# Folding layer 1's output weights in its first step, with the first queries made one item earlier

## The chip, the cores and the metric

The kernel runs on one core of a Trainium2 chip. The metric is the device time of one execution in microseconds (us). The engines are named as in the profile: PE is TensorE (matrix products), DVE is VectorE, ACT is ScalarE, POOL is GpSimd, SP is SyncE, which issues most of the DMA transfers. Each engine works through its own queue of instructions in order, and engines wait for each other through semaphores. PEclk is the clock that the throttle granted to TensorE, 1.00 being full speed.

## The reference

Two transformer layers on x of shape 2 x 1024 x 256, all in float32. Layer 0 is a 16-head attention with a ternary-weight FFN beside it. Layer 1 is a latent attention with its own FFN beside it; only that attention matters here. Cut to its core:

```python
q = rmsnorm(x @ wq_a.T) @ wq_b.T            # 16 heads: 128 plain + 64 rotated values
ckv = x @ wkv_a.T
kv, k_pe = rmsnorm(ckv[..., :64]), apply_rope(ckv[..., 64:])
w = wkv_b.reshape(16, 256, 64)
q_absorb, out_absorb = w[:, :128], w[:, 128:]
q_abs = einsum('bhsd,hdc->bhsc', q_nope, q_absorb)
scores = (q_abs @ kv + apply_rope(q_pe) @ k_pe) * SCALE    # causal softmax -> attn
x = einsum('bhst,btc->bhsc', attn, kv)
x = einsum('bhsc,hdc->bhsd', x, out_absorb)
return x.reshape(b, s, 16 * 128) @ wo.T
```

The last two products take no input but weights beside `x`, so `out_absorb` and `wo` can be multiplied with each other first, for each head: a 64 x 256 matrix. In the same way `wq_b` can be multiplied with `q_absorb`. The kernel calls this folding.

## The kernel before, in words

**Layers.** Layer 0 and everything that prepares layer 1 run under an order written out by hand. A list `fill` holds the pieces of the two FFNs, and a list `side` holds the pieces that prepare layer 1. The loop at L1076 takes one piece of `fill` and then one or more pieces of `side`, until both are empty. Each piece issues its matmuls and the copies that empty its PSUM bank. The pieces of `fill` that stand last are the FFN's products `up` (matmul L679) and `down` (twelve matmuls at L696 into one bank, which DVE adds to x at L701). Their banks come from a ring of three, `ps_m`, which the pieces of `side` use too.

**Preparation.** Among the pieces of `side` are, in this order near the end:

- `fold(p)` for the head pairs p = 0..7 (L818). Its loads come from SP two pieces ahead (`fold_load`, L799). Four matmuls at L825 fold the query weights, two at L833 fold the output weights (eight records in the profile for the first, four for the second); the results are copied out of two banks of `ps_m` by `copy_out`, which takes DVE and ACT in turn.
- `turn_keys` (L779), then `queries1` (L784), which turns four blocks of query latents with four matmuls at L791 and scales them on DVE at L792, out of one bank of `ps_m`.
- `query(k)` for k = 0, 1 (L1098), the queries of layer 1's first step. `project` (L139 and L146, 32 matmuls) writes two PSUM banks. `rotate` (L158) copies from there on ACT (L165, L153, L168), multiplies with cosine and sine (L169, L170) and adds the halves (four times L174), all of these six on POOL.

The last items of `side` are ordered as

```python
side += last[:2] + [lambda: query(0), last[2], lambda: query(1), last[3]]
```

where `last` are the four pieces of `queries1` for the second batch. Five pieces of `fill` (L696) come after the last of them.

**Layer 1's attention.** Its buffers (`att1`, and `ps1` in PSUM) lie in the memory that layer 0 leaves. It runs in 16 steps: a batch, a pair of blocks of 128 rows (i and 7 - i) and half of the heads. A step has four cycles c = 0..3. A cycle computes scores (matmul L1164, then DVE adds the mask and takes the maximum at L1171, then ACT takes the exponential at L1175), turns them over on DVE (L1181), computes a quarter of the product with the values for the step before (L1212), and in cycles 0 and 2 projects and rotates the queries of the next step. In cycles 1 and 3 come transposes (L1198) and the output product with the folded weights `wvo` (L1239) for the steps before. The first step has no step before it, so it has neither values nor output products; `wvo` is first read in the third step. PSUM holds two pairs of banks "s" for the scores and projections and four banks "o" for the values. Each step's turned weights lie in a tile `pT`, of which there are two buffers. The values need `vrep`, which 32 transfers from SP write (L1115) in x's place, after x with the first layer added has been written to memory (L703).

Of the kernel before, what the change touches and what calls it, by code (L numbers as in the profile page):

```python
# [46 lines left out]
def two_layers(ctx: ExitStack, tc: tile.TileContext, a: dict, out: bass.AP):  # L47
# [38 lines left out]
    def copy_out(dst, src, scale=None):  # L86

        turn[0] += 1
        if turn[0] % 2:
            if scale is None:  # L90
                nc.vector.tensor_copy(dst, src)
            else:
                nc.vector.tensor_scalar(dst, src, scale, None, ALU.mult)
        else:
            nc.scalar.activation(dst, src, AF.Copy, scale=1.0 if scale is None else scale)
# [94 lines left out]
    with ExitStack() as scope:  # L190
# [10 lines left out]
        def ps_bank():  # L201
            return ps0.tile([P, SC], F32, tag="m", name="ps_m", bufs=3)
# [596 lines left out]
        def fold_load(p):  # L799
            if p == 0:  # L800


                wm = main.tile([P, 2, NPAIR, P], F32, tag="wA", name="wm")
                folded["wm"], folded["w2"] = wm[:, 0], wm[:, 1]
                nc.sync.dma_start(folded["w2"][:R2], a["wpe2"])
                folded["wvo"] = main.tile([P, NPAIR, E], F32, tag="wB", name="wvo")
                folded["wo"] = l0.tile([P, 4, 2, E], F32, tag="ctx_n", name="fold_wo")
            t0 = l0t.tile([P, S], F32, tag="head0", name="fold0", bufs=3)
            t, at = {}, 0
            for key, width in (("wbn", LQ), ("wka", LKV), ("wva", LKV)):  # L810
                t[key] = t0[:, at : at + 2 * width].rearrange("p (h r) -> p h r", h=2)
                at += 2 * width
            t["wo"] = folded["wo"][:, p % 4]
            for key in ("wbn", "wka", "wva", "wo"):
                nc.sync.dma_start(t[key], a[key][:, 2 * p : 2 * p + 2, :])
            folded[p] = t

        def fold(p):  # L818
            if p + 2 < NPAIR:
                fold_load(p + 2)  # L820
            t = folded[p]
            pm = ps_bank()
            for lo, n, at in ((0, P, 0), (P, R2, P)):
                for hh in range(2):
                    nc.tensor.matmul(  # L825
                        pm[P - n :, at + hh * LKV : at + (hh + 1) * LKV],
                        t["wbn"][:, hh, lo : lo + n], t["wka"][:, hh, :], start=True, stop=True,
                    )
            copy_out(folded["wm"][:, p, :], pm[:, :P])
            copy_out(folded["w2"][R2:, p, :], pm[R2:, P : 2 * P])  # L830
            pv = ps_bank()
            for hh in range(2):
                nc.tensor.matmul(  # L833
                    pv[hh * LKV : (hh + 1) * LKV, :E], t["wva"][:, hh, :], t["wo"][:, hh, :],
                    start=True, stop=True,
                )
            copy_out(folded["wvo"][:, p, :], pv[:, :E])


        with tc.manual_schedule():  # L840

# [234 lines left out]
            while fill:  # L1076
                k = len(fill)
                pump()
                for _ in range(-(-len(side) // k)):
                    side.pop(0)()  # L1080
                if k == 17:
                    wpe = main.tile([P, 8 * E], F32, tag="wC", name="wpe")

                    maskw = wpe[:, NPAIR * P + 4 * P :]
                    trig = wpe[:, NPAIR * P : NPAIR * P + 4 * P].rearrange("p (k t) -> p k t", k=4)
                    wpe = wpe[:, : NPAIR * P].rearrange("p (r c) -> p r c", r=NPAIR)
                    nc.sync.dma_start(wpe, a["wpe"])
                    for k_, i in enumerate((TB - 1, 0)):
                        for x_, key in enumerate(("cosq", "sinq")):
                            nc.sync.dma_start(  # L1090
                                trig[:, 2 * k_ + x_], a[key][:, i * P : (i + 1) * P]
                            )

                    maskw = maskw.bitcast(BF16)
                    nc.gpsimd.memset(maskw[:, : S - P], 0.0)
                    nc.gpsimd.tensor_copy(maskw[:, S - P :], maskz[:, SC - P :])

                    def query(k):  # L1098
                        q = ready[steps[0]][k]
                        q.project(ps_pair())  # L1100
                        q.rotate(
                            room=[temp("t").rearrange("p (r t) -> p r t", r=QP) for _ in range(2)]
                        )

                    ahead(0)
                    last = [lambda c=c, n=n: queries1(1, c, n) for n in (0, 4) for c in range(2)]
                    side += last[:2] + [lambda: query(0), last[2], lambda: query(1), last[3]]
            while side:
                side.pop(0)()

# [20 lines left out]
    with ExitStack() as scope:  # L1131
# [9 lines left out]

        class Step:
            pass

        def new_step(b, i, g):
            s = Step()
# [108 lines left out]
        with tc.manual_schedule():  # L1255
            prev, older = None, None

            def values(n0, n1):
                for sb in range(n0, n1):
                    product(prev, sb)  # L1260

            for at in range(len(steps)):
                s = new_step(*steps[at])
                nxt = ahead(at + 1) if at + 1 < len(steps) else ()
                for c in range(NCY):
                    wide = [2 * c, 2 * c + 1]
                    share = (c * NSB // NCY, (c + 1) * NSB // NCY) if prev is not None else (0, 0)
                    if c == 0 and older is not None:
                        normalize(older, 0)
                        fetch_x(older)  # L1270
                    scores(s, 0, wide[:1])
                    if c == 0:
                        if older is not None:
                            normalize(older, 1)
                        if prev is not None:
                            inverse(prev)
                        scores(s, 0, wide[1:])
                        scores(s, 1, wide)
                        values(*share)
                    else:  # L1280
                        values(*share)
                        scores(s, 1, wide)
                        turn_over(s, 0, wide[0])
                        scores(s, 0, wide[1:])
                    k = c // 2
                    q, after = None, []
                    if c % 2 == 0:
                        if nxt:
                            q = nxt[k]
                            q.project(pair("t"))  # L1290
                    elif prev is not None:
                        t = pair("t")
                        if older is not None:
                            after.append(output(older, k, t[:, 0, :E]))
                        after.append(inverse_T(prev, k, t[:, 1]))
                    if c == 0:
                        turn_over(s, 0, wide[0])
                        turn_over(s, 0, wide[1])
                        turn_over(s, 1, wide[0])
                        turn_over(s, 1, wide[1])  # L1300
                    else:
                        turn_over(s, 1, wide[0])
                        turn_over(s, 1, wide[1])
                        for f in after:
                            f()
                        turn_over(s, 0, wide[1])
                    if q is not None:
                        q.rotate()
                older, prev = prev, s

            for k in range(2):
                normalize(older, k)
                if k == 0:
                    fetch_x(older)
            inverse(prev)
            mid = prev.nsb // 2
            values(0, mid)
            for k in range(2):
                t = pair("t")
                after = [output(older, k, t[:, 0, :E]), inverse_T(prev, k, t[:, 1])]  # L1320
                for f in after:
                    f()
                if k == 0:
                    values(mid, prev.nsb)
            normalize(prev, 0)
            mid = (prev.nsb + NSB) // 2
            values(prev.nsb, mid)
            t = pair("t")
            output(prev, 0, t[:, 0, :E])()
            values(mid, NSB)  # L1330
            normalize(prev, 1)
            t = pair("t")
            output(prev, 1, t[:, 0, :E])()
# [67 lines left out]
```

## Time and profile before

| | us |
|---|---|
| median of 3 runs | 1321.2 |
| lowest and highest | 1320.69, 1322.42 |
| the profiled execution, its own time | 1319.51 |
| its span, first to last instruction | 1317.4 |
| PE busy | 1268.4 (96%) |
| DVE busy | 744.2 (56%) |
| ACT busy | 641.3 (49%) |
| POOL busy | 487.2 (37%) |
| mean granted clock | 0.984 |

A line of the timeline gives the start, the duration, the engine, the line of the kernel, the operation with what it writes and reads, how many instructions it stands for, and in brackets how long the engine was idle before it and whose work ended that. A name with an arrow such as `ps_s<-kT,qc` reads "ps_s from kT and qc". A window's line gives each engine's busy time in that stretch, the granted clock, the DMA engines' mean share and their GB/s. The span counts from the first instruction; 2.1 us of the execution lie around it.

### The profile page before, as it was taken

How to read it: one execution, taken by the hardware profiler on the slowest of the kernel's cores; microseconds unless marked ns; L12 is line 12 of the kernel's file. 1: busy time of each engine (PE TensorE's matmuls, PEld its weight loads, DVE VectorE, ACT ScalarE, POOL GpSimd, SP SyncE). 2: the span in 40 equal slices, each digit the busy share in tenths (PEclk: the TensorE clock that was granted, in tenths of full speed). 3: DMA queues.
4: the chain of work that ended last, by engine and by line, in shares of the span. 5: the costliest groups of instructions: out<-in, count | busy, mean ns of one | idle time of the engine just before them, and what ended most of it. 6: DMA issues, size and time to landing. Idle time of an engine off the chain costs nothing. (4 is left out here: it accounts for less than half of the span.)

```text
span 1317.4 us, 36641 instructions
## 1 busy us (share of the span) xinstructions
PE 1268.4 (96%) x15790; PEld 797.0 (60%) x15790; DVE 744.2 (56%) x1873; ACT 641.3 (49%) x1227; POOL 487.2 (37%) x514
## 2 busy tenths in 40 slices
PE   7989999999999999999998889999999999999997
PEld 6445554544646544456576557777666667777665
DVE  5656454646555656125324567666657677666663
ACT  3455536556455433433324555555555555555541
POOL 5444315344324021113126344443444344443320
PEclk9889999999999999999999899999999999999999
DMA  7212300010101000002042200000000000000000
GB/s 227 56 41 65 104 10 17 9 25 1 25 1 25 1 25 20 17 1 78 1 130 58 32 18 11 24 13 6 27 11 26 7 27 11 26 11 6 23 6 23
DMA packets 65809, 41.12 MB, mean 31 GB/s; under 512 B 37840, under 2 KB 63184, under 8 KB 65392
## 3 DMA queue, kind: packets, MB, share of 16 engines
q1 hardware_dynamic: 64528, 35.25, 10.5%
q8 instruction: 124, 2.03, 0.6%
q0 software_dynamic: 416, 2.49, 0.5%
q10 hardware_dynamic: 704, 1.05, 0.3%
q14 instruction: 37, 0.30, 0.1%
HBM read 26.18 MB, written 10.49 MB: 28 GB/s over the span
## 5 line engine op out<-in xcount | busy, mean ns | idle before, releaser
L1175 ACT ACTIVATE p<-p,nmax 128x1024 f32<-128x1024 f32 (+7 forms) x256 | 197.2, 771 | 206.3 <-DVE nmax L1171 205.5
L1164 PE MATMUL ps_s<-kT,qc 128*128 128x512 f32 (+3 forms) x768 | 279.8, 499 | 14.2 <-DVE nmax L1171 13.0
L1171 DVE CUSTOM_DVE_ANT_0 p<-ps_s,wpe 128x1024 f32<-128x1024 f32 (+7 forms) x256 | 184.9, 744 | 185.5 <-PE ps_s L1164 180.3
L454 ACT ACTIVATE p<-ps_s 128x1024 f32<-128x1024 f32 (+1 forms) x192 | 153.3, 809 | 168.4 <-PE ps_s L447 163.3
L1164 PEld LDWEIGHTS ps_s<-kT,qc 128*128 128x128 f32 x768 | 131.4, 191 | 123.8 <-issue 90.9
L1181 DVE STREAM_TRANSPOSE pT<-p 128x1024 f32<-128x1024 f32 (+7 forms) x256 | 186.5, 758 | 13.2 <-ACT p L1175 13.2
L406 PE MATMUL ps_m<-head,head 16*128 16x512 f32 (+3 forms) x672 | 178.1, 537 | 1.7 <-DVE nmx L417 1.3
L447 PE MATMUL ps_s<-head,head 17*128 17x512 f32 (+3 forms) x768 | 166.2, 537 | 0.0
L1212 PE MATMUL ps_o<-pT,vrep 32*64 32x128 f32 x9216 | 151.3, 275 | 6.3 <-DVE xT L1222 3.7
L1212 PEld LDWEIGHTS ps_o<-pT,vrep 32*64 32x64 f32 x9216 | 134.8, 131 | 33.9 <-issue 25.5
L174 POOL TENSOR_TENSOR qc<-t,t 32x512 f32<-32x512 f32 x120 | 152.1, 1268 | 8.1
L457 POOL TENSOR_SCALAR_AFFINE_SELECT p<-p 128x256 f32<-128x256 f32 x128 | 53.4, 420 | 232.4 <-ACT p L454 231.8
L169 POOL TENSOR_TENSOR t<-t,cosq 128x512 f32<-128x512 f32 x28 | 35.7, 1273 | 259.8 <-issue 144.1
L406 PEld LDWEIGHTS ps_m<-head,head 16*128 16x128 f32 x672 | 67.3, 183 | 85.2 <-issue 29.0
L679 PE MATMUL ps_m<-xnT,w 128*128 128x512 f32 x192 | 93.9, 617 | 0.0
L422 DVE TENSOR_REDUCE nmx<-ps_m 128x1 f32<-128x512 f32 x112 | 72.2, 685 | 32.6 <-PE ps_s L447 24.4
L417 DVE CUSTOM_DVE_ANT_0 junk<-ps_m,maskz,nmx 128x512 f32<-128x512 f32 (+3 forms) x112 | 57.6, 548 | 46.9 <-PE ps_s L447 29.5
L472 PE MATMUL ps_o<-p,v 128*32 128x512 f32 (+3 forms) x768 | 81.6, 498 | 0.0
L560 PEld LDWEIGHTS ps_m<-wpr,hT 128*128 128x128 f32 x512 | 59.9, 191 | 17.9 <-DVE nmx L422 6.8
L417 DVE CUSTOM_DVE_ANT_0 junk<-ps_m,maskz 128x512 f32<-128x512 f32 (+3 forms) x112 | 50.4, 487 | 34.2 <-PE ps_s L447 31.5
L560 PE MATMUL ps_m<-wpr,hT 128*128 128x128 f32 x512 | 66.6, 282 | 0.0
L1239 PE MATMUL ps_t<-wvo,xT 128*128 128x256 f32 x256 | 62.7, 387 | 4.0 <-DVE nmax L1171 2.6
(180 smaller groups left out, 1756.6 us busy)
## 6 DMA issues: line engine op xcount, KB each, us to landing
stage<-rows SPq DMA_DIRECT2D x96, 64.0 KB, 3.2
rows<-proj SPq DMA_DIRECT2D x23, 256.0 KB, 2.2
w<-in_w SPq DMA_DIRECT2D x3, 768.0 KB, 5.0
x_sb<-in_x SPq DMA_DIRECT2D x4, 512.0 KB, 12.1
x<-x_sb SPq DMA_DIRECT2D x4, 512.0 KB, 3.0
fold_wo<-in_wo SPq DMA_DIRECT2D x8, 256.0 KB, 3.3
vrep<-kv SPq DMA_DIRECT2D x32, 64.0 KB, 2.1
xin<-x SPq DMA_DIRECT2D x16, 128.0 KB, 2.2
```

Of the source, the lines that this page charges most:

```text
L174: (even, odd)[x].tensor_tensor(self.qc[64 + 32 * x : 96 + 32 * x, hh], t1[at : at + 32], t2[at : at + 32], ALU.add,)
L406: nc.tensor.matmul(t[:, :w], quad(q, c, D0)[:, i * P : (i + 1) * P], quad(k, c, D0)[:, k0 : k0 + w], start=True, stop=True, tile_position= ...
L417: nc.vector.tensor_tensor_reduce(junk[:, :w], t[:, :w], maskz[:, SC - w :], -1.0, dst if k0 else 3.0e38, ALU.add, ALU.min, dst,)
L447: nc.tensor.matmul(t[:, c % 2, :w], quad(k, c, D0 + 1)[:, j * P : (j + 1) * P], quad(q, c, D0 + 1)[:, at : at + w], start=True, stop=True, ...
L454: nc.scalar.activation(p[:, pair[0] : pair[0] + 2, :w], t[:, :, :w], AF.Exp)
L560: nc.tensor.matmul(po[:, :P], f["h", hc // 2][:, hc % 2, t * P : (t + 1) * P], wpr[:, hc, cols], start=(hc == 0), stop=(hc == NH0 - 1),)
L679: nc.tensor.matmul(pw, w1t[f"w{i + 1}"][:, kc, hc * P : (hc + 1) * P], xnT1[n // 2][:, kc, (n % 2) * SC : (n % 2 + 1) * SC], start=(kc == ...
L1164: nc.tensor.matmul(sc[:, j * SC + n0 : j * SC + n1], s.q[k].qc[:, h // QP, h % QP, :], kT[:, s.b * S + n0 : s.b * S + n1], start=True, sto ...
L1171: nc.vector.tensor_tensor_reduce(p, sc[:, j * SC : j * SC + w], maskw[:, S - w :], -1.0, 3.0e38, ALU.add, ALU.min, nmax,)
L1175: nc.scalar.activation(p, p, AF.Exp, bias=nmax, scale=-1.0, accum_out=s.rsum[:, k, h : h + 1])
L1181: nc.vector.transpose(s.pT[:, at, h, :], s.p[k, h])
L1212: nc.tensor.matmul(s.o[64 * hh : 64 * hh + 64, c, k * P : (k + 1) * P], vrep[32 * c : 32 * c + 32, s.b * 32 + sb, :], s.pT[32 * c : 32 * c ...
```

## The change

Three things are changed. First, `fold` and `fold_load` lose the output weights: two matmuls, one bank and one copy in each of eight pieces, and two of the four loads. Second, a new function `output_weights` makes the same product within layer 1's first step. Its inputs go into the one buffer of `pT` that this step doesn't use, by five transfers (2.5 MB) issued from POOL. Its eight products go into the four banks "o", dealt out by `fill()` over cycles 1 to 3 (three, two, three), and two ACT copies at the step's end bring the result to `wvo`. Third, the two `query` pieces stand one piece earlier in `side`, and query 1's rotation has its two multiplies and the two odd additions on DVE, the two even additions on POOL.

```diff
@@ fold_load
-                folded["wvo"] = main.tile([P, NPAIR, E], F32, tag="wB", name="wvo")
-                folded["wo"] = l0.tile([P, 4, 2, E], F32, tag="ctx_n", name="fold_wo")
...
-            for key, width in (("wbn", LQ), ("wka", LKV), ("wva", LKV)):
+            for key, width in (("wbn", LQ), ("wka", LKV)):
...
-            t["wo"] = folded["wo"][:, p % 4]
-            for key in ("wbn", "wka", "wva", "wo"):
+            for key in ("wbn", "wka"):
                 nc.sync.dma_start(t[key], a[key][:, 2 * p : 2 * p + 2, :])
@@ fold
-            pv = ps_bank()
-            for hh in range(2):
-                nc.tensor.matmul(
-                    pv[hh * LKV : (hh + 1) * LKV, :E], t["wva"][:, hh, :], t["wo"][:, hh, :],
-                    start=True, stop=True,
-                )
-            copy_out(folded["wvo"][:, p, :], pv[:, :E])
@@ query
                         q.rotate(
+                            (
+                                (nc.gpsimd, nc.gpsimd, nc.gpsimd),
+                                (nc.vector, nc.gpsimd, nc.vector),
+                            )[k],
                             room=[temp("t").rearrange("p (r t) -> p r t", r=QP) for _ in range(2)]
                         )
...
-                    side += last[:2] + [lambda: query(0), last[2], lambda: query(1), last[3]]
+                    side += [last[0], lambda: query(0), last[1], lambda: query(1)] + last[2:]
@@ layer 1
+        def output_weights():
+
+            t = att.tile([P, NSB, NH2, 32], F32, tag="pT", name="wov", bufs=2)
+            t = t.rearrange("p n h q -> p (n h q)")
+            wo = t[:, : NH * E].rearrange("p (h e) -> p h e", h=NH)
+            wva = t[:, NH * E : NH * (E + LKV)].rearrange("p (h d) -> p h d", h=NH)
+            nc.gpsimd.dma_start(wva, a["wva"])
+            for h in range(0, NH, 4):
+                nc.gpsimd.dma_start(wo[:, h : h + 4], a["wo"][:, h : h + 4])
+            folded["wvo"] = main.tile([P, NPAIR, E], F32, tag="wB", name="wvo")
+            pv = ps.tile([P, 4, SC], F32, tag="o", name="ps_wvo").rearrange(
+                "p k (x e) -> p (k x) e", e=E
+            )
+
+            def product(p):
+                for hh in range(2):
+                    nc.tensor.matmul(
+                        pv[hh * LKV : (hh + 1) * LKV, p, :], wva[:, 2 * p + hh, :],
+                        wo[:, 2 * p + hh, :], start=True, stop=True,
+                    )
+
+            def take():
+                for k in range(0, NPAIR, 4):
+                    nc.scalar.copy(folded["wvo"][:, k : k + 4, :], pv[:, k : k + 4, :])
+
+            return [lambda p=p: product(p) for p in range(NPAIR)], take
@@ steps
+            fold, fold_take = output_weights()
+
+            def fill():
+                if c > 0 and fold:
+                    fold.pop(0)()
...
                         values(*share)
+                        fill()
                         scores(s, 1, wide)
+                        fill()
                         turn_over(s, 0, wide[0])
                         scores(s, 0, wide[1:])
+                        if c != 2:
+                            fill()
...
+                if at == 0:
+                    fold_take()
                 older, prev = prev, s
```

## The prediction

> **What bounds the kernel now.** First the page's busy shares and slices: TensorE (PE) is busy for 96% of the span, so only its idle or half-clock time, or work taken from it, can move the end.
>
> ```profile
> PE 1268.4 (96%) x15790; PEld 797.0 (60%) x15790; DVE 744.2 (56%) x1873; ACT 641.3 (49%) x1227; POOL 487.2 (37%) x514
> ...
> PE   7989999999999999999998889999999999999997
> ...
> PEclk9889999999999999999999899999999999999999
> ```
>
> Slices are 32.9 us. PE dips between 691 and 790 us, and the granted clock falls to 0.8 in the slice from 724: the seam between the layers. There I read the timeline by engine, PE first:
>
> ```profile
> 656.32 0.75 PE L825 MATMUL ps_m<-fold 128*128 128x64 f32 x5
> 656.82 0.43 PE L833 MATMUL ps_m<-fold_wo,fold 128*64 128x256 f32 x1
> 656.91 0.34 PE L825 MATMUL ps_m<-fold 128*64 128x64 f32 x3
> 657.09 0.60 PE L833 MATMUL ps_m<-fold_wo,fold 128*64 128x256 f32 x3
> 657.62 1.98 PE L679 MATMUL ps_m<-xnT,w 128*128 128x512 f32 x4
> ...
> 697.44 0.60 PE L791 MATMUL ps_m<-ident,qa 128*128 128x128 f32 x4
> 697.87 6.86 PE L696 MATMUL ps_m<-w,hid 128*128 128x128 f32 x60
> 705.21 3.67 PE L1164 MATMUL ps_s<-kT,qc 128*128 128x512 f32 x8 [0.47 <-DVE x_sb L701]
> ...
> 726.39 3.78 PE L1164 MATMUL ps_s<-kT,qc 128*128 128x512 f32 x4 [2.90 <-DVE nmax L1171]
> ```
>
> Up to 704.7 PE has no gap: a matmul removed there is time removed. Behind it, the step's first cycle waits. The same timeline on GpSimd (POOL) and VectorE (DVE), and the windows, say for what:
>
> ```profile
> 703.58 5.21 POOL L174 TENSOR_TENSOR qc<-t 32x512 f32<-32x512 f32 x4
> ...
> 708.82 1.23 DVE L1171 CUSTOM_DVE_ANT_0 p<-ps_s,wpe 128x1024 f32<-128x1024 f32 x1 [3.76 <-POOL qc L174]
> ```
>
> ```profile
> 708.55:711.96 3.41, 1.75 (x17) 1.23 (x18) 3.14 (x9) 1.87 (x3) 0.24 (x1) 1.00 0.59 185
> 711.96:715.37 3.41, 3.41 (x22) 3.19 (x19) 2.33 (x4) 1.29 (x6) 0.00 (x0) 0.50 0.50 99
> 715.37:722.20 6.83, 6.22 (x21) 2.99 (x20) 3.57 (x8) 4.89 (x11) 3.04 (x3) 1.00 0.64 98
> 722.20:725.61 3.41, 1.21 (x6) 0.52 (x4) 2.52 (x6) 1.24 (x2) 3.25 (x3) 1.00 0.64 100
> 725.61:732.44 6.83, 6.05 (x21) 3.29 (x22) 4.04 (x11) 2.91 (x7) 1.27 (x1) 0.50 0.62 96
> ```
>
> Columns: stretch, length, busy PE, PEld, DVE, ACT, POOL, then granted clock. A window with PE busy for half its time or less is followed by half clock. The second query's rotation on POOL ends at 708.8, and DVE's first softmax pass (L1171) waits for it though its scores were done near 707.1.
>
> **What the Trainium skill says.** "TensorE: Matmul & The Clock Gate", Part 1: The HAM clock gate: activity in windows decides between full and half rate. The trace agrees: clock 0.50 in stretches of 3.41 us or twice that, after windows busy 1.75 and 1.21 of 3.41. "GPSIMD Engine Reference", 1. Specifications: POOL shares its SBUF interfaces with DVE instructions that have two SBUF inputs. Agrees: a DVE multiply of two SBUF tiles takes 684 ns as a median, but 1,647 with a POOL instruction in flight:
>
> ```profile
> L317 DVE TENSOR_TENSOR q_th<-q_ab,q_sg x8: 657/684/1647, 17.1 to 132.2; 128x512 f32<-128x512 bf16 x8
> ```
> "DMA: Bandwidth & Descriptors", Anatomy of one DMA — SWDGE (gpsimd) path: about 2.0 us plus bytes/436 GB/s. For 1 MB that is 4.4 us; the trace's 1 MB load from this queue took 8.5 beside others.
>
> **The change part by part**, in the clock of the kernel before.
>
> *Fold without output weights.* Out of a gapless PE go four L833 records in each of eight items. The next item would start 0.35 to 0.43 us sooner (657.62 against about 657.25; column halves overlap). 8 × 0.37 = **−3.0** (−2.9 to −3.4). The eight PSUM copies (0.43 on DVE, 0.38 on ACT) and 16 SyncE loads go too, worth nothing: those engines wait there, and SP's copies hide behind PE.
>
> *Queries one item sooner, half of the second's turn on DVE.* The project of query 1 now ends near 694.3 (696.26 − 1.8), the ACT copies at 697.4 (they end 2.95 later). DVE then holds L169, L170 and two L174, and behind them in its queue L701, which empties a bank of the three-deep ring `ps_m`. PE passes L696, L791 and L696 by 697.4 and stops at the last but one L791, whose bank that L701 frees. Prices: no row shows these ops on DVE; the nearest, DVE tensor_tensor 128x512, is 0.65 to 0.69, so four take 2.5 or more, plus 0.29 for L701. With no wait for the port PE stops 2.8 us; with one POOL L174 (1.26, and about 0.55 of switching) in between, 4.1, which I take, because POOL adds query 0 from about 694 and then query 1's even halves; alternating after each op 5.5 to 6.7. A stop above half a window brings half clock for one window or so: 1.6 more on the 6.7 us of L696 that remain (up to 2.5). **+5.7** (2.8 to 8.5). POOL meanwhile ends query 1 by about 703, before layer 0 does.
>
> *First step.* Now DVE waits for scores, not POOL: 1.75 sooner (708.82 to 707.1). The project from 711.25 ran at half clock (4.57 against 3.0): at full clock the scores for DVE's pass at 717.74 come 0.85 sooner still, by when DVE itself has only just done its transposes. The eight products, each about 0.5 us as L833, fall into PE's idle time (2.90 at 723.5) and raise the 1.21 of 3.41 window to 2.2 or more, so scores at 726.39 (3.78 against 1.85) and the project behind (4.15 against 3.0) go at full clock: 3.1. Step 1's values at 745.43 (3.73 against 2.32): 1.4. Sum −7.1; one window in such a seam staying at half costs up to 1.7, which I charge at 0.7: **−6.4** (−4.2 to −7.3). The products cost nothing while hidden by this idle time, 4 us if it were gone. The closing ACT copies (two of about 1.02, as L454) fit between query copies and the next exponential by my reading; uncovered they are 2.0.
>
> *Loads.* 2.5 MB on POOL's queue start at layer 0's end T0 (the tile lies in layer 0's memory); the first product, ahead of the scores that now start near 715 (717.7 − 2.6), needs `wva` and the first quarter of `wo` about T0+10.3. Estimate from the skill's price and issues of 0.54 (POOL's first loads in the trace): 1.3 + 2.0 + 2.4 = T0+5.7 for this first MB alone, or T0+8.7 if all five share the engines evenly: hidden. Later quarters are needed at T0+13.8, +17, +28. POOL issues them before step 1's turn, which waits at 719 anyway. SP's next `cosq` load waited for POOL's turn until 708.82, now for the last L696: SP's queue behind it, the x1 write and 32 `vrep` loads, starts some 4 us sooner; they ended at 734 and are needed at 745. They and the new loads share bandwidth.
>
> Sum: −3.0 + 5.7 − 6.4 = **−3.7**. Profiled, 1319.5 becomes 1315.8 (span 1317.4 to 1313.7; 2.1 lie around it); the median of the runs shown is 1.7 higher: **1317.5**.
>
> **Rivals.** (A) As above, 1315.5 to 1319.
>
> (B) POOL and DVE alternate on the port: the stop is 5.5 to 6.7, half clock lasts longer; −3.0 + 7.4 − 6.4 = −2.0, or 0 with the seam's half-clock windows left: 1319.2 to 1321.5. For it: L317's 1,647 ns. Against: DVE instructions queued back to back kept the port in layer 0 while POOL's L270 waited.
>
> (C) No contention: the stop is 2.8, partly below the clock's threshold: −5.5 to −7: 1314 to 1315.7.
>
> (D) Slower: the loads come late to the first product. PE is in order, so scores queue behind it, DVE and ACT behind these; each us late is a us. It decides from 3.7 us late (T0+14), and from 6.3 (T0+16.6) it is measurably slower: about 1324 to 1326. For it: loads of 0.25 MB on this queue needed 11 us at the start. Against: those stood behind 2.3 MB of others.
>
> (E) The seam stays: DVE's first pass isn't released by the POOL halves alone, or the half-clock windows only shift; −3.0 + 5.7 − 2.5: 1321.4.
>
> **How the numbers follow.** A 48%, B 22%, C 11%, D 14% (other late waits at the step's end included), E 5%. A measurement of this kernel tells about 0.2%, 2.6 us, from no change. Faster (below 1318.6): most of A (45), C (11), a little of B (1). Slower (above 1323.8): D but for a part (13), the ends of B and E (3). The rest is the same. The range runs from within C to within D, 1313.8 to 1323: left out are most of D and the tip of C. A alone has 1315.5 to 1319.
>
> **What would show it.** L833's rows gone from the fold items, with periods of 2.7 instead of 3.11. A PE idle of 3 to 5 us released by DVE L701 near 694 to 697 in the new profile, DVE rows L169, L170, L174 of 0.65 or more beside it, and a 0.50 window after. DVE's first softmax pass released by PE. No idle above 1 us before the products. Clock 1.00 through most of the first step. I am wrong if DVE's four ops are far from 2.5 to 4 us in sum, if the product records wait for DMA, or if the idle before score matmuls in the first step stays near 2.9.

## The result, and the profile after

| | before | after |
|---|---|---|
| median of 12 runs, us | 1319.12 | 1318.55 |
| lowest to highest, us | 1313.98 to 1322.89 | 1315.86 to 1324.14 |
| profiled execution, its own time, us | 1319.51 | 1317.95 |
| its span, us | 1317.4 | 1316.0 |
| mean granted clock in it | 0.984 | 0.988 |

The ratio of after to before is 1.0001, with a 95% interval from 0.9983 to 1.0018: no difference that can be measured. Most of the distance from the predicted 1317.5 to the first median of 1321.2 was never there, since with more runs the kernel before stands near 1319.

The page of the changed kernel (busy times, then two of the rows with 40 slices):

```profile
PE 1265.2 (96%) x15790; PEld 795.9 (60%) x15790; DVE 747.4 (57%) x1873; ACT 641.8 (49%) x1225; POOL 485.5 (37%) x515
...
PE   7989999999999999999998999999999999999997
...
PEclk9789999999999999999999999999999999999999
```

The dip in the clock near 724 us is gone. PE dipped in three slices from 691 to 790 us; now it dips in the first of them alone, the one that holds layer 0's end. The PE timeline of the changed kernel shows the steps of the prediction one by one (L822 is the old L825, L1155 the new products, L1185 and L1192 are the old L1164 and L1171, L1233 the old L1212):

```profile
655.35 0.93 PE L822 MATMUL ps_m<-fold 128*128 128x64 f32 x8
656.21 1.98 PE L679 MATMUL ps_m<-xnT,w 128*128 128x512 f32 x4
658.03 0.93 PE L822 MATMUL ps_m<-fold 128*128 128x64 f32 x8
...
698.35 1.08 PE L791 MATMUL ps_m<-ident,qa 128*128 128x128 f32 x4 [5.20 <-DVE x_sb L701]
699.22 8.12 PE L696 MATMUL ps_m<-w,hid 128*128 128x128 f32 x60
707.82 4.12 PE L1185 MATMUL ps_s<-kT,qc 128*128 128x512 f32 x12 [0.48 <-DVE x_sb L701]
...
717.61 0.65 PE L1155 MATMUL ps_wvo<-wov 128*64 128x256 f32 x4
...
726.41 1.98 PE L1185 MATMUL ps_s<-kT,qc 128*128 128x512 f32 x4 [0.70 <-DVE nmax L1192]
...
742.61 2.32 PE L1233 MATMUL ps_o<-pT,vrep 32*64 32x128 f32 x144
```

A fold item and the piece of L679 behind it now take 2.68 us (655.35 to 658.03) where they took 3.11: 8 × 0.43 = 3.4 saved. Then PE stands still for 5.20 us, released by L701. In the first step the idle of 2.90 has become 0.70, the products stand without a wait, and the values run at full clock. The timelines of VectorE and of GpSimd in the changed kernel show what held L701 up:

```profile
693.04 0.87 DVE L169 TENSOR_TENSOR t<-t,wpe 128x512 f32<-128x512 f32 x1 [5.75 <-ACT t L168]
693.84 1.75 DVE L170 TENSOR_TENSOR t<-t,wpe 128x512 f32<-128x512 f32 x1
695.62 2.35 DVE L174 TENSOR_TENSOR qc<-t 32x512 f32<-32x512 f32 x2
698.01 0.29 DVE L701 SCALAR_TENSOR_TENSOR x_sb<-ps_m,x_sb 128x128 f32<-128x128 f32 x1
...
709.91 1.22 DVE L1192 CUSTOM_DVE_ANT_0 p<-ps_s,wpe 128x1024 f32<-128x1024 f32 x1 [2.23 <-PE ps_s L1185]
```

```profile
689.44 5.60 POOL L174 TENSOR_TENSOR qc<-t 32x512 f32<-32x512 f32 x4
695.73 3.37 POOL L174 TENSOR_TENSOR qc<-t 32x512 f32<-32x512 f32 x2 [0.69 <-DVE t L170]
```

VectorE's four instructions last from 693.04 to 697.97, 4.9 us, and L701 stands right behind them. The multiply L170 took 1.75 while GpSimd was still adding the first query (689.44 to 695.04); the two additions took 2.35 while GpSimd made its own two, which took 3.37. VectorE's first softmax pass is now released by PE, with 2.23 of idle instead of 3.76. The windows of the changed kernel (busy PE, PEld, DVE, ACT, POOL, then the granted clock):

```profile
691.60:695.01 3.41, 1.55 (x14) 1.36 (x12) 1.97 (x2) 1.36 (x3) 3.28 (x3) 1.00 0.00 0
695.01:698.43 3.42, 0.08 (x1) 0.08 (x2) 3.34 (x5) 0.00 (x0) 2.67 (x3) 1.00 0.00 0
698.43:701.85 3.42, 3.42 (x17) 3.42 (x18) 1.47 (x3) 0.00 (x0) 0.67 (x1) 0.50 0.00 0
...
1288.93:1292.34 3.41, 1.22 (x85) 1.25 (x92) 2.20 (x5) 0.58 (x1) 1.05 (x2) 1.00 0.22 68
1292.34:1295.76 3.42, 3.42 (x97) 2.91 (x82) 0.00 (x0) 0.00 (x0) 0.12 (x1) 0.50 0.17 52
```

The stop costs a window at half clock behind it. Another falls into the kernel's tail, where the traced execution of before stayed at full clock.

The sum over the seam, from these two executions: the fold −3.4; the stop and its half clock +6.9 (5.20 + 3.42/2); from the last L696 to the project after step 1's first values 44.35 us before (704.74 to 749.09) and 37.52 after (707.34 to 744.86), −6.8. Together −3.3. Ahead of the fold PE of the changed kernel was already 0.97 us early (655.35 against 656.32), and not by the change: the execution of before had a window at half clock from 493.51 to 496.92, in a part that the change leaves alone, and this one had none there. So the lead behind the seam is 4.2 us (749.09 to 744.86). Matched matmul by matmul, it shrinks to 2.4 by 1290 us, in small shifts of the steps between, and the window in the tail takes 1.6 of that, of which 0.7 comes back. At the end the span is 1.4 shorter.

### The profile page after: what moved, and what is told of

Read it like the earlier page. It is cut to its first block, busy times and chain, and to the rows that moved or that the text cites. A ratio compares the mean times of both kernels' runs of the same rounds, so it can differ in the third digit from the quotient of the medians.

```text
span 1316.0 us, 36626 instructions
## 1 busy us (share of the span) xinstructions
PE 1265.2 (96%) x15790; PEld 795.9 (60%) x15790; DVE 747.4 (57%) x1873; ACT 641.8 (49%) x1225; POOL 485.5 (37%) x515
## 5 line engine op out<-in xcount | busy, mean ns | idle before, releaser
L1192 DVE CUSTOM_DVE_ANT_0 p<-ps_s,wpe 128x1024 f32<-128x1024 f32 (+7 forms) x256 | 185.2, 745 | 180.4 <-PE ps_s L1185 179.0
L1185 PE MATMUL ps_s<-kT,qc 128*128 128x512 f32 (+3 forms) x768 | 278.0, 497 | 8.6 <-DVE nmax L1192 7.5
L1185 PEld LDWEIGHTS ps_s<-kT,qc 128*128 128x128 f32 x768 | 130.8, 190 | 116.2 <-issue 89.4
L1233 PE MATMUL ps_o<-pT,vrep 32*64 32x128 f32 x9216 | 150.9, 275 | 6.5 <-issue 2.8
L174 POOL TENSOR_TENSOR qc<-t,t 32x512 f32<-32x512 f32 x120 | 152.2, 1268 | 8.1
L1233 PEld LDWEIGHTS ps_o<-pT,vrep 32*64 32x64 f32 x9216 | 134.6, 131 | 33.8 <-issue 25.4
L169 POOL TENSOR_TENSOR t<-t,cosq 128x512 f32<-128x512 f32 x28 | 35.6, 1272 | 260.0 <-issue 144.2
L679 PE MATMUL ps_m<-xnT,w 128*128 128x512 f32 x192 | 92.3, 608 | 0.0
```

Source lines behind the costliest of these rows:

```text
L174: (even, odd)[x].tensor_tensor(self.qc[64 + 32 * x : 96 + 32 * x, hh], t1[at : at + 32], t2[at : at + 32], ALU.add,)
L1185: nc.tensor.matmul(sc[:, j * SC + n0 : j * SC + n1], s.q[k].qc[:, h // QP, h % QP, :], kT[:, s.b * S + n0 : s.b * S + n1], start=True, sto ...
L1192: nc.vector.tensor_tensor_reduce(p, sc[:, j * SC : j * SC + w], maskw[:, S - w :], -1.0, 3.0e38, ALU.add, ALU.min, nmax,)
L1233: nc.tensor.matmul(s.o[64 * hh : 64 * hh + 64, c, k * P : (k + 1) * P], vrep[32 * c : 32 * c + 32, s.b * 32 + sb, :], s.pT[32 * c : 32 * c ...
```

## The experiments

Theory S: the change is two gains and one loss of the same size. The fold and the sooner queries gain; the half turn on VectorE (half of query 1's rotation, called its turn below) holds L701, so a bank of `ps_m`, so PE. Theory N, the rival: what is won in the seam comes back as half clock elsewhere, whatever stands at layer 0's end. Ratios are to the kernel before on the same chip, with 95% intervals.

**e1_turn_on_pool: the change without the half turn on VectorE.**

```diff
                         q.rotate(
-                            (
-                                (nc.gpsimd, nc.gpsimd, nc.gpsimd),
-                                (nc.vector, nc.gpsimd, nc.vector),
-                            )[k],
                             room=...
```

> The changed kernel with the second query's turn all on GpSimd, as before the change; the fold in the first step and the queries one item sooner stay. Theory S (the half turn on VectorE holds up L701 and so TensorE: 5.2 us idle and one window at half clock, about 6.9 us): that stop is gone, the L696 items run without a gap, GpSimd ends the second turn about 702.6, about when the first head's scores are done (702.8), so nothing waits for it; 1309 to 1312 us, 7 to 10 below before. Rival N (the gains of the seam are undone by half-clock windows elsewhere, whatever stands in layer 0's end): within 3 us of before. Rival W (GpSimd's turn is late and VectorE waits for it as before): 1313 to 1316, with an idle of 1 us or more on VectorE released by L174.

Measured: 1311.28, ratio 0.9941 (0.9919 to 0.9963). A repetition, with this expectation:

> The kernel of e1_turn_on_pool once more: 6 to 10 us below before. Above 1315 would say that the first comparison was lucky.

gave 1313.32, 0.9952 (0.9932 to 0.9973): 5.9 us below the median of before on that chip (1319.22), just short of the 6 to 10 expected. From the PE timeline of e1, and from VectorE's:

```profile
699.58 4.18 PE L1181 MATMUL ps_s<-kT,qc 128*128 128x512 f32 x12 [0.47 <-DVE x_sb L701]
...
709.60 0.65 PE L1151 MATMUL ps_wvo<-wov 128*64 128x256 f32 x4 [0.17 <-DMA wov<-in_wo]
```

```profile
701.76 1.23 DVE L1188 CUSTOM_DVE_ANT_0 p<-ps_s,wpe 128x1024 f32<-128x1024 f32 x1 [2.33 <-PE ps_s L1181]
```

Layer 0 ends without a stop, and VectorE's first pass still waits for PE alone: GpSimd's whole second turn was hidden already, so moving half of it bought nothing. Rival W's sign, a wait for L174, is absent. The one edit is worth 0.5 to 0.6% (1.0001 − 0.9941, and from the repetitions 1.0003 − 0.9952). Theory N falls.

**e2_fold_alone and e4_sooner_alone: each gain by itself.** e2 is e1 with the order of the queries of before; e4 is the kernel before with the new order.

```diff
-                    side += last[:2] + [lambda: query(0), last[2], lambda: query(1), last[3]]
+                    side += [last[0], lambda: query(0), last[1], lambda: query(1)] + last[2:]
```

> Only the fold moved into the first step; queries and turn as in the kernel before. Theory S: the fold saves 3.4 us in layer 0 and its products fill part of the first step's idle time and keep the clock up (up to 4.5 more): 1311.5 to 1315.5. VectorE still waits about 3.8 us for GpSimd's L174 at the start of the step. Rival N: no difference from before that can be measured.

> The kernel before with the queries one item sooner alone, the turn on GpSimd. Theory S: no stop in layer 0; GpSimd ends the second turn about 706.8, so VectorE's first softmax pass is released by the scores instead (1.75 us sooner), and the clock windows decide the rest: 1315.5 to 1318, 1.5 to 3.5 below before. Rival N: no difference.

Measured: e2 1314.15, 0.9975 (0.9960 to 0.9990); e4 1316.03, 0.9980 (0.9964 to 0.9996). Both lie in the ranges of S, e4's gain only just clear of none. In e2 VectorE still waits for GpSimd:

```profile
706.43 1.23 DVE L1188 CUSTOM_DVE_ANT_0 p<-ps_s,wpe 128x1024 f32<-128x1024 f32 x1 [3.73 <-POOL qc L174]
```

0.25% and 0.20% make 0.45%, next to the 0.48 and 0.59% of both together.

**e3_queries_both: both edits of the queries, the fold left in layer 0.**

```diff
                         q.rotate(
+                            (
+                                (nc.gpsimd, nc.gpsimd, nc.gpsimd),
+                                (nc.vector, nc.gpsimd, nc.vector),
+                            )[k],
...
+                    side += [last[0], lambda: query(0), last[1], lambda: query(1)] + last[2:]
```

> The kernel before with the queries one item sooner and half the second turn on VectorE, the fold left in layer 0. Theory S: TensorE stops 5 us at the last but one L791 and a window at half clock follows, against 1.75 to 3.4 gained in the first step: 1322 to 1325, slower by 3 to 6. Rival N: within 2 us of before.

Measured: 1324.81, 1.0053 (1.0037 to 1.0068). The stop is the same, on PE:

```profile
701.79 1.11 PE L791 MATMUL ps_m<-ident,qa 128*128 128x128 f32 x4 [5.18 <-DVE x_sb L701]
```

Against e4 the half turn costs 0.73%, 9.6 us; in the changed kernel, against e1, 0.5 to 0.6% (6.7 to 8.2 us). The stop and one or two windows at half clock account for 6.9 to 8.6. The traced e3 has one such window more (731.05 to 734.47, behind the first step's idle of 2.90), which the trace of e4 lacks.

**after_again: the changed kernel once more.**

> The changed kernel once more, beside the others of this call. Theory S (the fold and the sooner queries win 7.8, the half turn on VectorE costs as much): within 2.5 us of before. In its profile a stop of about 5.2 us released by L701 and one or two windows at half clock near it, and a first step without such a window. Rival N (luck of the executions): a median 3 us or more below before would say that the first comparison was unlucky.

Measured: 1318.64, 1.0003 (0.9987 to 1.0018), with a stop of 5.21 and two windows at half clock behind it. The first comparison was no accident.

**e5_first_query_earlier: the half turn without GpSimd's work beside its first part.**

```diff
-                    side += [last[0], lambda: query(0), last[1], lambda: query(1)] + last[2:]
+                    side += [lambda: query(0)] + last[:2] + [lambda: query(1)] + last[2:]
```

> The changed kernel with the first query one more item sooner; the second query and its half turn on VectorE stay where the change put them. GpSimd then ends the first query's turn near 693, when VectorE's half turn starts. Theory P (half of the stop is waits for GpSimd's instructions in flight): VectorE's four instructions take 3.3 to 3.9 us instead of 5.0, the stop is 3.5 to 4.1, and the time is about 1.3 below the changed kernel's. Rival C (the four instructions cost this much on VectorE by themselves): they take 5.0 us still and the stop is 5.2.

VectorE's and PE's timelines:

```profile
693.44 0.69 DVE L169 TENSOR_TENSOR t<-t,wpe 128x512 f32<-128x512 f32 x1 [5.75 <-ACT t L168]
694.05 0.68 DVE L170 TENSOR_TENSOR t<-t,wpe 128x512 f32<-128x512 f32 x1
694.77 2.36 DVE L174 TENSOR_TENSOR qc<-t 32x512 f32<-32x512 f32 x2
```

```profile
697.50 0.66 PE L791 MATMUL ps_m<-ident,qa 128*128 128x128 f32 x4 [3.95 <-DVE x_sb L701]
```

The multiplies fall from 0.87 and 1.75 to 0.69 and 0.68 when GpSimd is idle (its first turn ended at 693.3); the additions, which GpSimd's still stand beside, stay at 2.36. The stop falls to 3.95, as theory P said, and rival C falls. So of the 4.9 us about 1.2 are the multiplies' waits for GpSimd, and about 1.0 those of the additions, if these would take 0.69 each alone as the multiplies do. The time, 1317.57, 0.9999 (0.9975 to 1.0023), is too uncertain to show the 1.3.

**e10_multiplies_only: VectorE takes the two multiplies alone.**

```diff
-                                (nc.vector, nc.gpsimd, nc.vector),
+                                (nc.vector, nc.gpsimd, nc.gpsimd),
```

> The changed kernel with the two multiplies of the second turn on VectorE and all four additions on GpSimd. Theory S (TensorE stops for as long as VectorE is held, less 0.1 or so): VectorE is held 2.6 us and L701 takes 0.29, the stop is 2.6 to 2.9; with a window at half clock behind it or not, 2.3 to 4 below the changed kernel: 1314.5 to 1316.5. Rival O (a stop of any length costs the window at half clock and most of the rest): within 1 us of the changed kernel.

PE's timeline, and the window behind:

```profile
697.53 0.65 PE L791 MATMUL ps_m<-ident,qa 128*128 128x128 f32 x4 [2.68 <-DVE x_sb L701]
```

```profile
698.48:701.90 3.42, 3.42 (x18) 3.42 (x17) 0.80 (x2) 0.00 (x0) 3.25 (x4) 0.50 0.00 0
```

VectorE is held from the start of L169 to the end of L701 for 5.26 us in the changed kernel, 4.01 in e5 and 2.74 here; the stop is 0.06 shorter each time (5.20, 3.95, 2.68). Even the shortest is followed by half clock. Measured 1316.45, 0.9981 (0.9961 to 1.0002): what S said, but the interval reaches to the changed kernel's 1.0003, so the time by itself doesn't exclude rival O.

**e6_no_products: the products left out.** In e1 the eight products and the two closing copies are gone, and GpSimd sets the folded weights to zero.

```diff
+            nc.gpsimd.memset(folded["wvo"], 0.0)
-            return [lambda p=p: product(p) for p in range(NPAIR)], take
+            return [], lambda: None
```

> The kernel of e1_turn_on_pool with the eight products of the output weights and the two copies left out; the folded weights are set to zero by GpSimd, so the output product adds nothing. The loads stay. Theory H (the products fill TensorE's idle time of the first step and cost nothing, and they help to keep the clock up): the same as e1 or up to 3 us slower, with an idle of about 2.9 us in the first step. Rival T (they cost TensorE's time): 2 to 4.7 us faster than e1.

Measured: 1313.17, 0.9968 (0.9948 to 0.9987). Leaving them out gains nothing, so T falls: the products cost nothing that can be measured. The idle they had filled is back in PE's timeline:

```profile
732.72 1.98 PE L1182 MATMUL ps_s<-kT,qc 128*128 128x512 f32 x4 [2.90 <-DVE nmax L1189]
```

That they also keep the clock up isn't shown: this execution has no half clock in its seam all the same, and the interval overlaps e1's.

**e7_loads_reversed: the first product waits for all 2.5 MB.**

```diff
-            nc.gpsimd.dma_start(wva, a["wva"])
-            for h in range(0, NH, 4):
+            for h in range(NH - 4, -1, -4):
                 nc.gpsimd.dma_start(wo[:, h : h + 4], a["wo"][:, h : h + 4])
+            nc.gpsimd.dma_start(wva, a["wva"])
```

> The kernel of e1_turn_on_pool with the five loads issued in reverse order, so that the first product waits for all 2.5 MB. It waits about 5 us longer. Theory D (what is late at the first product is late at the end): 5 to 7 us slower than e1, so 1316 to 1318. Rival K (the first step has slack, since VectorE and ScalarE set it): less than 2.5 us slower than e1.

PE's timeline at the first product:

```profile
724.34 1.12 PE L1151 MATMUL ps_wvo<-wov 128*64 128x256 f32 x4 [4.96 <-issue]
```

"issue" means that the view names no releaser; the last of the five loads, `wva`, landed at 724.14, 10.4 us after its issue at 713.78, and the product follows at once. Measured: 1319.53, 1.0008 (0.9988 to 1.0027), 0.56 to 0.67% above e1: 7.4 to 8.8 us for a wait of 5.0, more than the 5 to 7 of theory D. Its profile has two windows at half clock there (722.77 to 729.59), worth 3.4. So lateness at the first product does come out at the end, as the prediction's rival D had it, and costs more than a us for each us. The margin is thin: in e1 the first product waited 0.17 already.

**e9_both_earlier: both queries one place sooner than in e1.**

```diff
-                    side += [last[0], lambda: query(0), last[1], lambda: query(1)] + last[2:]
+                    side += [lambda: query(0), last[0], lambda: query(1)] + last[1:]
```

> The kernel of e1_turn_on_pool with both queries half an item sooner still (each ahead of the piece of queries1 that it followed), all of the turn on GpSimd. GpSimd then ends about 700.8 - 1.8 = 699, when layer 0 ends, and the loads of the output weights start some 2 us sooner, so the first product no longer waits for them (0.17 us in e1_turn_on_pool). Theory S (GpSimd's turn is already hidden in e1): the same as e1 within 2 us, about 1310. Rival M (the margin of the loads counts in most executions): 2 to 4 us below e1.

Measured: 1312.38, 0.9951 (0.9929 to 0.9973): as e1, whose interval it shares, and the product's wait for its load is gone. Rival M falls. e1 and e9 are faster than both kernels.

**before_again: the kernel before, for its windows.**

> The kernel before once more, for its windows. Theory R (its idle stretches in the first step fall into the clock's windows differently from one execution to the next): the profile shows another number of half-clock windows between 705 and 750 than the four of the first profile, with the same idle of 3.8 us on VectorE and 2.9 us on TensorE. Rival A (they are always there): four windows again.

Measured: 1318.42, 0.9989 (0.9956 to 1.0021). Its windows, and two of e4, which has the same idle of 2.90 between 721.67 and 724.58:

```profile
722.46:725.88 3.42, 1.16 (x6) 0.52 (x4) 2.53 (x6) 1.24 (x2) 3.23 (x4) 1.00 0.62 97
725.88:732.70 6.82, 6.10 (x22) 3.35 (x23) 3.98 (x11) 2.97 (x7) 1.25 (x1) 0.50 0.59 91
```

```profile
719.74:723.15 3.41, 1.87 (x7) 0.71 (x5) 2.52 (x5) 1.24 (x2) 3.20 (x4) 1.00 0.63 101
723.15:726.57 3.42, 1.99 (x6) 0.75 (x6) 2.47 (x8) 1.95 (x6) 1.89 (x2) 1.00 0.61 95
```

Four windows at half clock again, as rival A had it. But the windows lay at the same place against the program within 0.3 us (711.96 and 712.22 begin one), so the two are hardly two draws. The Trainium skill ("TensorE: Matmul & The Clock Gate", Part 1: The HAM clock gate) says that the window runs free of the kernel's start; the profiles fit that, their first half-clock stretch beginning anywhere from 27.98 to 31.32 us. In e4 the same idle is cut in two by a boundary, PE is busy for 1.87 and 1.99, and no half clock follows. So where a boundary cuts an idle stretch matters. But the share of a window that PE is busy doesn't decide alone: windows with 1.55 (the changed kernel, from 691.60) and 1.62 (e4, from 736.81) were followed by full clock, one with 1.62 (before, from 742.68) by half.

The timed executions leave no trace, so only their mean clock tells of such windows. The 198 of before that the ratios use have a median clock of 0.987, where both profiles had 0.984; the 34 of the changed kernel have 0.988. (1 − clock) × span is the clock time lost: 21.1 us in the first profile, 17.1 in the median execution, 15.8 after. Medians by bands of clock, e1 with its repetition:

| clock (executions of the three) | before, us | after, us | e1, us |
|---|---|---|---|
| 0.983 to 0.985 (42, 9, 2) | 1321.6 | 1322.3 | 1318.6 |
| 0.986 to 0.988 (83, 14, 14) | 1318.3 | 1318.3 | 1313.6 |
| 0.989 to 0.992 (57, 9, 18) | 1314.7 | 1316.9 | 1311.1 |

At an equal clock the change wins nothing; e1 wins 3 to 5 us. (In the last band part of the difference is the clock itself, a mean of 0.990 before and 0.989 after.)

## Why the prediction was right or wrong

The time lies within the range and near the number, but the gain of 3.7 us that it stood for did not come. That the number is near is luck: it was counted from 1321.2, and from the 1319.12 of more runs the same gain gives 1315.4. Both sides of the sum lean the wrong way. The interval of e1 is some 3 us to either side, that of the half turn wider: that no gain of 3.7 is left is shown, how the miss divides between the two rows is an estimate.

| | predicted, us | timed runs, us |
|---|---|---|
| fold and first step, without the stop | −9.4 (−3.0 − 6.4) | −6.3 to −7.8 (e1 and its repetition) |
| half turn on VectorE | +5.7 | +6.7 to +8.2 (changed kernel against e1) |
| sum | −3.7 | about 0 |

Point by point:

- *Fold.* −3.0, with −3.4 at the end of its range; it was 3.4 in the trace. Right, and e2's 0.25% (3.3 us) agrees.
- *The stop.* Releaser and chain were as described: L791 behind L701 behind four instructions of VectorE. (It is the last L791; the prediction wrote the last but one.) Its length was mis-sized: 4.1 for one wait for GpSimd, against 5.20, and 6.9 with its half clock against 5.7. The step that failed is "with one POOL L174 (1.26, and about 0.55 of switching) in between, 4.1, which I take": VectorE waited at L170 and, by the estimate from e5, again at the additions, which is near rival B's mechanism, priced at 5.5 to 6.7. (The 0.55 isn't in the 4.1, which is 2.8 and 1.26; and 696.26 − 1.8 is 694.5, from which the 697.4 follows.) VectorE's four instructions took 4.9 us, outside the 2.5 to 4 that the prediction had named as a sign of being wrong. That a stop brings half clock held for every one measured, from 2.68 to 5.21 us: two windows in after_again and e3, one in the first profile, e5 and e10.
- *First step.* −6.4, in the traces −6.8: VectorE's first pass released by PE, products without a wait, no half clock. As a reading of that profile it was right. As time it seems priced too high: take the fold's 3.4 from e1's gain, and 2.9 to 4.4 us are left for it, an estimate. By the prediction's own terms about 4.7 of the 6.4 are windows at half clock (0.85 + 3.1 + 1.4 − 0.7; the 4.15 in it is 4.04 in the timeline, 730.10 to 734.14). The step in doubt is taking the windows of one profile for those of the median execution, which by its mean clock lost 17.1 us and not 21.1. That is an argument and not shown: the profiled execution's own time, 1319.51, was near the median all the same.
- *Behind the seam.* The prediction put this at nothing. In the two traces 2.8 us of PE's lead went there, 1.8 in steps that the change leaves alone and 1.0 over the tail.
- *Loads.* Estimated from the price in the Trainium skill ("DMA: Bandwidth & Descriptors", Anatomy of one DMA — SWDGE (gpsimd) path), T0+5.7 for the first megabyte alone or T0+8.7 for an even share. In the changed kernel the first of the four `wo` loads, issued at 708.60, took 7.5 us and landed at 716.1, which is T0+8.7 (T0 is 707.34): the even share. The product came at T0+10.3. Hidden, but by some 1.5 us.
- *Closing copies.* 1.93 us on ACT at 739.47, followed by 0.55 of idle: hidden, as said.
- *Rivals.* The median lies in A's range; as a difference from before, the outcome is B's (−2.0 to 0), by the waits for GpSimd and by a first step worth less than priced. D didn't happen, and e7 shows its price. C fell with the waits for GpSimd. E's first reason fell, since VectorE's pass was released by PE; its second, half clock that only shifts, fits the window in the tail.

What stays open: in which stretches the timed executions lose their clock, and what decides, beside the share of a window, whether half clock follows.

## What to carry to other kernels

Before moving work to an engine that looks idle, list what is queued behind it there and whose buffer that frees: here half a turn, already hidden on GpSimd, held a copy that empties PSUM for 5 us, and a change worth half a per cent came to nothing. Price a multiply of two SBUF tiles on VectorE, while GpSimd works beside it, at its contended duration (here 1.75 us, not 0.68). And before counting a half-clock window as a gain, compare the profiled execution's mean clock with that of the timed ones.

## What the runs showed of the hardware that was not expected

- Additions of 32x512 on VectorE and GpSimd side by side: two took 2.35 us on VectorE and two 3.37 on GpSimd, where GpSimd alone takes 1.26 each. What VectorE alone would take for them no run shows.
- The clock can fall without an idle window ahead. In nine of the fourteen profiles one window at half clock begins between 491 and 506 us, in layer 0, behind a window in which PE was busy all the time (3.42 of 3.42 in before, ahead of 493.51). In e6 and e7, 17.1 us at half clock stand in layer 0, which no kernel here changes before its end; the windows of e7:

```profile
316.58:320.00 3.42, 3.08 (x23) 2.39 (x21) 1.66 (x6) 2.17 (x4) 0.46 (x2) 1.00 0.00 0
320.00:337.06 17.06, 17.06 (x82) 9.96 (x82) 4.74 (x18) 4.14 (x6) 2.32 (x5) 0.50 0.00 1
```

PE is busy for 90% of the window before and for all of the five that follow, yet the clock stays at half. The execution took 1326.16 us where the kernel's median is 1319.53. Its cause is not known.
